# Seven block products for queries and outputs in three attentions, another order of VectorE's work, and weight loads spread over the attentions

## The chip, the cores and the metric

The kernel runs on one core of a Trainium2 chip. The metric is the device time of one execution in microseconds; the time of a version is the median of its runs. The five engines have their names from the profile: PE (TensorE, matmuls; PEld is its weight load), DVE (VectorE), ACT (ScalarE), POOL (GpSimd) and SP (SyncE, which issues most transfers).

## What is computed

Four layers, each of an attention to a fixed context and a feed-forward part, on `x` of 4 batches x 256 tokens x 256 features; the context is 4 x 512 x 128. All is float32. The change concerns the attentions of layers 1, 2 and 3, which are alike:

```python
q = (x @ Wq).reshape(B, 256, 16, 128)          # 16 heads of 128
k = (ctx @ Wk).reshape(B, 512, 8, 128)         # 8, each for two heads
v = (ctx @ Wv).reshape(B, 512, 8, 128)
attn = softmax(einsum('bhtd,bhsd->bhts', q, k) / sqrt(128))
x = x + einsum('bhts,bhsd->bhtd', attn, v).reshape(B, 256, 2048) @ Wo
```

where the `x` in front of `Wq` is layer-normalised. The feed-forward parts are: routed low-rank vectors ("arrows") in layer 0; eight experts, two per token, and a shared one in layer 1; one of two networks per token in layer 2; and in layer 3 a network for the 64 tokens of each batch that a router picks.

## The kernel before

**Folded weights.** `folding` (line 957) multiplies, for each head, Wq with Wk into `m_sb` (256 x 128, as two blocks of 128 rows) and Wv with Wo into `n_sb` (128 x 256). A query is then `m` times the normalised x and is compared with the context itself; the weighted sum of the context times `n` is the output. For each pair of heads it issues eight matmul instructions `pm` (L968), a copy by ACT, the squares of `m` (for a bound on the scores: on POOL with a sum on VectorE for layer 1, on ACT for layers 2 and 3), `pn` (L989) and a copy by VectorE (L992).

**An attention** (line 1674) has 32 units: 4 batches b times 8 pairs of heads hp. The order of work on PE, ACT, DVE and POOL is written out by hand: the engines take their instructions in the order of the program. SP's order is left to the scheduler. In iteration n:

- `queries` of unit n+1 (L1689): for each of 2 heads, two matmuls of 128x128 weights on 256 tokens into one PSUM bank; ACT copies the 128x512 result (L1697).
- `heads` of unit n: four score matmuls of 512 columns (L1704), each followed by ACT's exponential (L1707); four matmuls with the context (L1710); ACT's copy `oT` (L1714); POOL adds two halves of the exponentials (L1717, `half`).
- `quotients`, at hp 1 for the second half of the batch before and at hp 5 for the first half of this one: a matmul `pz` (L1734), VectorE's reciprocal `rz`, and for each of four units VectorE's broadcast `wide` (L1747) and POOL's multiplication of `oT` in place (L1751).
- `summed` of the same unit n: VectorE adds the halves, transposes in blocks of 32 and reduces (L1723, L1725, L1729).
- `output` of the batch before, at hp 3: for each of two token blocks sixteen matmuls of 256 columns (L1760), and VectorE's addition to `x_sb` (L1768).
- `after`: work of the feed-forward part for the batch before, a step at hp 4, 5, 6 and 7 (norm, normalised tokens, transposes, choice of experts; in layer 3 the router, whose matmul `pw`, L2443, takes `diag` from VectorE, L2436).

The norm for the next batch is taken at hp 2, its tokens at hp 4 and its transposes at hp 6. The last batch's outputs stand behind the loop.

PSUM has eight banks in this stage: four for scores (tag "s"), two for "mm" (queries, outputs, folding), one for "o" and one for "t" (transposes, `pz`, small products of the router).

**Loads.** A layer's feed-forward weights are asked for as a block once the raw attention weights have been issued (`issue_after`), at the start of each attention; raw weights of the next attention are issued as four groups at once in the feed-forward part, by `load_raw` (line 941), into pools of two to four buffers.

**Between layers 1 and 2**, experts write their rows to DRAM (`yd`), and class `Back` (line 2162) gathers two rows for each token by indirect transfers of POOL (L2169), which VectorE adds to `x_sb` (L2177). One `Back` is asked for in each step of the folding, with four buffers; the norm of the next attention stands at the fourth step.

**Layer 0's last part** (loop at about line 1617) handles eight blocks of tokens ("arrows"): `routes` on VectorE (L1407 to L1418) with a product on POOL (L1419), transposes (L1427) and outputs (L1436, L1440), the folding of layer 1 in between, and the squares of the context (L1646, L1647).

Of the kernel before, what the change touches and what calls it, by code (L numbers as in the profile page):

```python
# [835 lines left out]
def bounded_path(ctx: ExitStack, tc: tile.TileContext, t, out: bass.AP, over):  # L836
# [30 lines left out]
    def load_fw(tag, shape, parts, name, pool=None):  # L867
        w = (pool or fwp).tile(shape, F32, tag=tag, name=name)
        for dst, src in parts(w):
            nc.sync.dma_start(dst, src)  # L870
        return w

# [68 lines left out]
    def load_raw(L, i):  # L941
# [4 lines left out]
        nc.sync.dma_start(wq_t, wq[h0 * P : (h0 + 4) * P, :].rearrange("(h e) d -> e h d", e=P))  # L946
        wk_t = rawp.tile([P, 2, DC], F32, tag="wk_t", name=f"wk_{L}_{i}")
        nc.sync.dma_start(wk_t, wk[g0 * P : (g0 + 2) * P, :].rearrange("(g e) c -> e g c", e=P))
        wv_t = rawp.tile([P, 2, DC], F32, tag="wv_t", name=f"wv_{L}_{i}")
        nc.sync.dma_start(wv_t, wv[g0 * P : (g0 + 2) * P, :].rearrange("(g e) c -> e g c", e=P))  # L950
        wo_t = rawp.tile([P, 4, D], F32, tag="wo_t", name=f"wo_{L}_{i}")
        done["raw"] = nc.sync.dma_start(
            wo_t, wo[h0 * P : (h0 + 4) * P, :].rearrange("(h e) d -> e h d", e=P)
        ).ins
        raws[L, i] = wq_t, wk_t, wv_t, wo_t

    def folding(L, m_sb, n_sb, on_act=False):

        for i in range(4):
# [4 lines left out]
            for g in range(2):  # L964
# [13 lines left out]
                if on_act:  # L978
                    for h in range(2):
                        nc.scalar.activation(  # L980
                            m2[:, :, h, :], m_sb[:, :, h1 + h, :], AF.Square,
                            accum_out=msq[:, L - 1, h1 + h : h1 + h + 1],
                        )
                else:
                    nc.gpsimd.tensor_tensor(
                        m2, m_sb[:, :, h1 : h1 + 2, :], m_sb[:, :, h1 : h1 + 2, :], ALU.mult
                    )
# [5 lines left out]
                if not on_act:  # L993
                    nc.vector.tensor_reduce(
                        msq[:, L - 1, h1 : h1 + 2], m2.rearrange("p d h c -> p h d c"), AX.XY, ALU.add
                    )
# [21 lines left out]
    with tc.manual_schedule(engines={E.PE, E.Activation, E.DVE, E.Pool}):  # L1018
# [597 lines left out]

        for n in range(B * NC):
            if n + 2 < B * NC:
                arrows[n + 2].routes()
            arrows[n].turned()  # L1620
# [7 lines left out]
            else:  # L1628
# [4 lines left out]
                for _ in range((0, 0, 1, 1, 2, 2, 1, 1)[n]):  # L1633
                    next(fold)
                if n + 3 < B * NC:
# [6 lines left out]
            if 2 <= n < 2 + B:  # L1642
# [4 lines left out]
                nc.vector.tensor_reduce(csq[:, b * NK : (b + 1) * NK], c2, AX.X, ALU.add)  # L1647
# [4 lines left out]
    fwp = ctx.enter_context(tc.tile_pool(name="fwp", bufs=1))  # L1652
# [26 lines left out]

# [1003 lines left out]
```

## Time and profile before

| what | us |
|---|---|
| median of 3 runs | 1537.04 (1534.7 to 1539.55) |
| the profiled execution's own time | 1532.39 |
| its span, first to last instruction | 1530.6 |
| PE busy | 1481.0 (97%) |
| DVE, ACT, POOL busy | 644.9, 589.1, 474.8 |
| VectorE's `summed`: addition, transpose, reduction, 96 each | 782, 711, 686 ns each |
| VectorE's broadcast L1747, 96 | 699 ns each |
| POOL's `half` L1717, 96 | 2344 ns each |
| POOL's division L1751, 90 | 1375 ns each |
| ACT's copies L1697 and L1714, 96 each | 585 ns each |

A row of a group of instructions reads: line, engine, operation, output<-inputs, shape, count, then busy time in us and the mean of one in ns, then the idle time of the engine ahead of them and what ended most of it. Durations of matmuls overlap, since a matmul starts before the one ahead has drained; the distance from start to start is what one costs. The view of waits names engine, line and what it waited for, with the total in us, how often, and the longest. The timeline has start in us, length in us, engine, line. The granted clock is TensorE's, as a share of full speed; over the whole span it was 0.988.

### The profile page before, as it was taken

The page shows a single profiled execution, that of the slowest core. Times are in us where ns is not written, and L with a number is a line of the kernel's source. Part 1 is how long each engine was busy: PE and PEld are TensorE (multiplying, and loading weights), DVE is VectorE, ACT ScalarE, POOL GpSimd, SP SyncE. Part 2 cuts the span into 40 slices and gives each one's busy share as a digit, 9 for nine tenths or more (in the row PEclk, how much of TensorE's full clock was granted, in tenths as well). Part 3 has the DMA queues.
Part 4 walks back from the last instruction along what each step waited for, and adds up shares of the span by engine and source line. Part 5 has one row for each costly group of instructions (what it writes and reads, how often), then busy time and mean ns, then how long its engine had stood idle before and what let it go on. Part 6 is the DMA issues. An engine that isn't in the chain of part 4 may idle for free.

```text
span 1530.6 us, 16401 instructions
## 1 busy us (share of the span) xinstructions
PE 1481.0 (97%) x6243; PEld 935.2 (61%) x6243; DVE 644.9 (42%) x1357; ACT 589.1 (38%) x1047; POOL 474.8 (31%) x354
## 2 busy tenths in 40 slices
PE   8999998999999999999999999999999999999997
PEld 7665676556565567656455656566885565565656
DVE  5666863233534435424233332425442334324363
ACT  4666332442434433234444342422234433423221
POOL 2222343243434331324244342423002343423330
PEclk9999999999999999999999999999999999999999
DMA  4000223100000003135000000000410000000000
GB/s 159 1 1 2 69 69 126 16 0 0 7 1 7 0 3 115 56 86 163 7 0 1 0 1 0 1 0 3 140 55 1 0 1 0 0 1 1 0 0 31
DMA packets 39955, 43.15 MB, mean 28 GB/s; under 512 B 3833, under 2 KB 36826, under 8 KB 39868
## 3 DMA queue, kind: packets, MB, share of 16 engines
q1 hardware_dynamic: 36892, 35.85, 7.4%
q0 software_dynamic: 1872, 5.11, 1.2%
q8 instruction: 52, 0.85, 0.2%
q10 hardware_dynamic: 1104, 1.05, 0.2%
q14 instruction: 35, 0.29, 0.1%
HBM read 36.89 MB, written 5.11 MB: 27 GB/s over the span
## 4 chain that ended last, share of the span: by engine, by line
PE 84%; DVE 9%; POOL 3%; issue 2%; ACT 1%; DMA 0%; POOLq 0%; DVEq 0%; ACTq 0%
PE ps L1704 20%; PE po L1710 20%; PE pq L1689 10%; PE py L1760 10%; PE ph L2308 2%; PE po L2345 2%; PE pgu L2130 2%; PE ps L1313 2%; PE po L1323 2%; PE pyf L1440 1%; POOL oT L1751 1%; PE pyr L2155 1%; PE paf L1390 1%; DVE wide L1747 1%; POOL yg L2169 1%
## 5 line engine op out<-in xcount | busy, mean ns | idle before, releaser
L1717 POOL TENSOR_TENSOR half<-pT 128x1024 f32<-128x1024 f32 x96 | 225.0, 2344 | 579.1 <-ACT pT L1707 406.9
L1704 PE MATMUL ps<-qT,cT 128*128 128x512 f32 x768 | 350.1, 599 | 3.8 <-ACT qT L1697 3.8
L1710 PE MATMUL po<-pT,c_sb 128*128 128x512 f32 x768 | 345.3, 592 | 0.0
L1707 ACT ACTIVATE pT<-ps,mbias 128x512 f32<-128x512 f32 x384 | 263.3, 687 | 77.9 <-PE ps L1704 68.0
L1710 PEld LDWEIGHTS po<-pT,c_sb 128*128 128x128 f32 x768 | 146.0, 190 | 183.6 <-issue 183.1
L1704 PEld LDWEIGHTS ps<-qT,cT 128*128 128x128 f32 x768 | 147.7, 193 | 149.7 <-issue 140.6
L1723 DVE TENSOR_TENSOR half<-half 128x512 f32<-128x512 f32 x96 | 75.0, 782 | 357.4 <-POOL half L1717 357.4
L1689 PE MATMUL pq<-xnT_a,m_sb 128*128 128x256 f32 x768 | 183.4, 383 | 0.7 <-ACT xnT_a L923 0.7
L1760 PE MATMUL py<-n_sb,oT 128*128 128x256 f32 x768 | 169.3, 380 | 1.3 <-POOL oT L1751 1.3
L1689 PEld LDWEIGHTS pq<-xnT_a,m_sb 128*128 128x128 f32 x768 | 143.6, 191 | 39.8 <-issue 14.1
L1760 PEld LDWEIGHTS py<-n_sb,oT 128*128 128x128 f32 x768 | 145.4, 190 | 26.1 <-issue 4.8
L1714 ACT COPY oT<-po 128x512 f32<-128x512 f32 x96 | 56.2, 585 | 263.4 <-PE po L1710 263.4
L1697 ACT COPY qT<-pq 128x512 f32<-128x512 f32 x96 | 56.1, 585 | 255.5 <-PE pq L1689 246.5
L1751 POOL TENSOR_TENSOR oT<-oT,wide 128x512 f32<-128x512 f32 x90 | 121.0, 1375 | 67.3 <-DVE wide L1747 67.3
L1317 ACT ACTIVATE pT<-ps 128x512 f32<-128x512 f32 x128 | 66.1, 603 | 40.8 <-PE ps L1313 40.6
L1747 DVE STREAM_TRANSPOSE wide<-rz 128x512 f32<-128x512 f32 x96 | 65.1, 699 | 28.8 <-POOL oT L1751 28.0
L1725 DVE STREAM_TRANSPOSE turned<-half 128x512 f32<-128x512 f32 x96 | 68.3, 711 | 4.8
L1729 DVE TENSOR_REDUCE sums<-turned 128x16 f32<-128x512 f32 x96 | 65.8, 686 | 3.3
L1743 DVE TENSOR_SCALAR rz<-pz 128x64 f32<-128x64 f32 x24 | 5.4, 224 | 137.1 <-PE pz L1734 137.1
L1768 DVE TENSOR_TENSOR x_sb<-x_sb,py 128x256 f32<-128x256 f32 x24 | 10.1, 421 | 115.9 <-PE py L1760 115.9
L2110 POOL DMA_INDIRECT xg<-xd,who x23 | 22.0, 956 | 59.3 <-PE pxg L2118 33.0
L1313 PE MATMUL ps<-qT,kT 16*128 16x256 f32 x512 | 38.6, 408 | 0.0
(343 smaller groups left out, 1511.3 us busy)
## 6 DMA issues: line engine op xcount, KB each, us to landing
wo<-in_L_wo SPq DMA_DIRECT2D x13, 512.0 KB, 7.1
wq<-in_L_wqT SPq DMA_DIRECT2D x12, 512.0 KB, 4.1
yd<-yr SPq DMA_DIRECT2D x23, 128.0 KB, 1.7
w<-in_F_w SPq DMA_DIRECT2D x2, 1024.0 KB
wgu<-in_F_wgT SPq DMA_DIRECT2D x1, 1760.0 KB, 6.9
wgu<-in_F_wuT SPq DMA_DIRECT2D x1, 1760.0 KB, 10.8
wk<-in_L_wkT SPq DMA_DIRECT2D x12, 128.0 KB, 4.2
wv<-in_L_wvT SPq DMA_DIRECT2D x12, 128.0 KB, 5.9
```

The lines of the kernel that those rows point to most:

```text
L1313: nc.tensor.matmul(ps[j][:, k, :], lhsT=kTs[b][r, hg, k0 : k0 + P], rhs=qTs[b][r, hg, :], start=True, stop=True)
L1317: nc.scalar.activation(pT[kp][:, j], ps[j], AF.Exp)
L1689: nc.tensor.matmul(pq[:, j, :], lhsT=m_sb[:, d, 2 * hp + j, :], rhs=xnTs[b][:, d, :], start=(d == 0), stop=(d == ND - 1),)
L1704: nc.tensor.matmul(ps, lhsT=cT[:, b, k * P : (k + 1) * P], rhs=qTs[b, hp], start=True, stop=True)
L1707: nc.scalar.activation(pT[:, k, :], ps, AF.Exp, bias=mbias[:, b, k : k + 1])
L1710: nc.tensor.matmul(po, lhsT=c_sb[:, b, k, :], rhs=pT[:, k], start=(k == 0), stop=(k == NK - 1))
L1717: nc.gpsimd.tensor_tensor(half, pT[:, 0:2], pT[:, 2:4], ALU.add)
L1723: nc.vector.tensor_tensor(part, half[:, 0], half[:, 1], ALU.add)
L1725: nc.vector.transpose(turned.rearrange("p f i -> p (f i)"), part)
L1747: nc.vector.transpose(wide, rz[:, i, :, None].to_broadcast([P, NB, 32]))
L1751: eng.tensor_tensor(oT, oT, wide.rearrange("p f i -> p (f i)"), ALU.mult)
L1760: nc.tensor.matmul(pys[c], lhsT=outs[b][h // 2][:, t0 : t0 + P], rhs=n_sb[:, h, :], start=(h == 0), stop=(h == H - 1),)
```

## The change

**Seven products.** A product of 2x2 blocks is made with seven block products and sums of blocks, by the scheme of Strassen and Winograd. For queries the blocks are the two 128-row halves of `m` for two heads and two halves of features and of tokens of x; for outputs the two heads and two token blocks of `oT`, and two heads and two feature halves of `n`. Sums of the weights are made once per attention, in its first batch (`m_sums` on VectorE, `n_sums` on POOL, four additions of 128x128 each per head pair), sums of x once per batch (`x_sums`, VectorE), sums of `oT` per unit (`o_sums`, POOL). The fourth of the additions is in place in most cases. The first two units of each attention keep the old form (`first_queries`), and so do the outputs of the last four head pairs of the last batch (`last_output`).

```diff
+            def s_sums(eng, a11, a12, a21, a22, s1, s2, s4):
+                eng.tensor_tensor(s1, a21, a22, ALU.add)
+                eng.tensor_tensor(s2, s1, a11, ALU.subtract)
+                eng.tensor_tensor(s4, a12, s2, ALU.subtract)
+                eng.tensor_tensor(a21, a11, a21, ALU.subtract)
...
+            def seven(of, u, tag="mm", between=None):
+                ps = []
+                for n, which in (("a", (1, 6, 7, 5)), ("b", (2, 3, 4))):
+                    if n == "b" and between:
+                        between()
+                    p = bank(tag, [P, len(which), P], f"p{n}{u}")
+                    for k, pair in enumerate(of):
+                        for at, i in enumerate(which):
+                            lhsT, rhs = pair[i]
+                            nc.tensor.matmul(
+                                p[:, at, :], lhsT=lhsT, rhs=rhs,
+                                start=(k == 0 and at == 0), stop=(k == len(of) - 1 and i == which[-1]),
+                            )
+                    ps.append(p)
+                return ps
+            def four(w, pa, pb):
+                nc.scalar.copy(w[:, 0, :], pa[:, 0, :])
+                nc.vector.tensor_tensor(w[:, 1, :], w[:, 0, :], pa[:, 1, :], ALU.add)
+                nc.vector.tensor_tensor(w[:, 2, :], w[:, 1, :], pa[:, 2, :], ALU.add)
+                nc.vector.tensor_tensor(w[:, 1::2, :], w[:, 1:3, :], pa[:, 3:4, :].to_broadcast([P, 2, P]), ALU.add)
+                nc.vector.tensor_tensor(w[:, 0:3, :], w[:, 0:3, :], pb, ALU.add)
```

The query takes both "mm" banks, an output group two of the four "s" banks. An output group is now four head pairs of one batch (one set of quotients).

**Order in an iteration.** The sums of exponentials of unit n-1 stand before the heads of unit n. Quotients stand at hp 4 (first half of the batch) and hp 0 (second half of the batch before); two divisions each follow at the next two iterations; the output group at the one after.

```diff
+                if n == 0:
+                    first_queries(1)
+                    x_sums(0)
+                elif n + 1 < len(units):
                     queries(*units[n + 1])
+                if b + 1 < B and hp == 6:
+                    x_sums(b + 1)
+                if b == 0:
+                    m_sums((hp + 2) % (H // 2))
+                if n:
+                    summed(*units[n - 1], half)
+                last, i = ((b, 0), hp - 4) if hp >= 4 else ((b - 1, 1), hp)
+                prev = last[0] >= 0
+                h0 = 4 * last[1]
+                if prev and i >= 2:
+                    for k in (2 * i - 4, 2 * i - 3):
+                        o_sums(last[0], h0 + k, nc.gpsimd)
                 half = heads(b, hp)
+                if prev and i == 0:
+                    quotients(*last)
+                if prev and i in (1, 2):
+                    for k in (2 * i - 2, 2 * i - 1):
+                        divided(last[0], h0 + k, nc.gpsimd)
+                if b == 0:
+                    n_sums(hp)
+                if prev and i == 3:
+                    out = Output(*last)
+                    if last != (B - 1, 0):
+                        out.products()
+                        out.add()
                 if after:
                     after(b, hp)
-            output(B - 1, 0, 0, H // 2)
-            quotients(B - 1, 1, last=True)
+            summed(*units[-1], half)
+            out.products(lambda: quotients(B - 1, 1))
+            for k in range(4):
+                divided(B - 1, 4 + k, nc.vector if k % 2 else nc.gpsimd)
+            out.add()
             if at_end:
                 at_end()
-            output(B - 1, 1, 0, H // 2)
-            for c in range(NC):
-                output(B - 1, c, H // 2)
+            last_output(B - 1)
```

The norm of the next batch moves from hp 2, 4 and 6 to hp 1, 3 and 5.

**Loads.** Feed-forward weights are put on a list, and one of them (up to five from the fifth head pair on in layers 2 and 3) is issued on SP after each unit of the first batch, behind ACT's copy of that unit. The down weights of the experts, `wd1` and `wd2`, are issued behind attention 1. Raw weights of layer 2 are issued behind the copies of blocks 2, 8 and 14 of the experts, and a last one after them; of layer 3, two at the start and two behind an addition of batches 0 and 1.

```diff
+    def load_waiting(n=1):
+        for dst, src in waiting[:n]:
+            behind(nc.sync.dma_start(dst, src), done["head"])
+        del waiting[:n]
...
+                if j in (2, 8, 14):
+                    load_raw(2, j // 6, done["slots"])
+            load_raw(2, 3)
```

**Around the attentions.** All squares of `m` are made on ACT; the sum of the context's squares is taken an iteration later; the routes of the last arrow stand behind the folding of iteration 5. Six of eight `Back` are asked for ahead of the folding, the last two after the norm, with eight buffers. ACT's function tables are loaded ahead of their use in three places.

```diff
-            if n + 2 < B * NC:
+            if n + 2 < B * NC and n != 5:
                 arrows[n + 2].routes()
...
+                if n == 5:
+                    arrows[7].routes()
...
+            nc.scalar.preload_act_table_set("exp_and_others")
+            for n in range(N8 - 2):
+                backs[n] = Back(n)
             for n in range(N8):
-                backs[n] = Back(n)
...
+                    for k in (N8 - 2, N8 - 1):
+                        backs[k] = Back(k)
```

## The prediction

> **What bounds the kernel now.** I read the page first, for which engine fills the span, then the groups of instructions, for what fills that engine, then the waits of TensorE, for the rest.
>
> ```profile
> span 1530.6 us, 16401 instructions
> PE 1481.0 (97%) x6243; PEld 935.2 (61%) x6243; DVE 644.9 (42%) x1357; ACT 589.1 (38%) x1047; POOL 474.8 (31%) x354
> ```
>
> ```profile
> L1704 PE MATMUL ps<-qT,cT 128*128 128x512 f32 x768 | 350.1, 599 | 3.8 <-ACT qT L1697 3.8
> L1710 PE MATMUL po<-pT,c_sb 128*128 128x512 f32 x768 | 345.3, 592 | 0.0
> L1689 PE MATMUL pq<-xnT_a,m_sb 128*128 128x256 f32 x768 | 183.4, 383 | 0.7 <-ACT xnT_a L923 0.7
> L1760 PE MATMUL py<-n_sb,oT 128*128 128x256 f32 x768 | 169.3, 380 | 1.3 <-POOL oT L1751 1.3
> ```
>
> TensorE is the bound; no other engine passes 42%. The queries (L1689) and the outputs (L1760), which the change recasts, are 384 matmuls each, shown as x768: a float32 matmul runs as two instructions. Their durations overlap (383 ns each, yet 183.4/768 = 239 ns of busy time), so I price by starts, in the timeline:
>
> ```profile
> 505.58 1.89 PE L1689 MATMUL pq<-xnT_a,m_sb 128*128 128x256 f32 x8
> 507.31 3.60 PE L1704 MATMUL ps<-qT,cT 128*128 128x512 f32 x8
> ...
> 1141.15 1.05 PE L968 MATMUL pm<-wk,wq 128*128 128x128 f32 x8
> 1142.05 1.02 PE L989 MATMUL pn<-wo,wv 128*128 128x512 f32 x2
> ```
>
> Eight instructions of 256 columns take 507.31 - 505.58 = 1.73 us, 216 ns each. L968 has just the shape that the change uses, 128x128 times 128x128 with new weights each time: 0.90 us for eight, 112 ns each. So half the columns cost 0.52 of the time, and a scheme that needs 7/8 of the columns gains less than an eighth. The waits of TensorE are short but not nothing:
>
> ```profile
> PE pw L2443 <- DVE diag L2436: 7.3, 4, 2.8
> PE pn L989 <- DVE n_sb L992: 4.0, 2, 3.8
> PE ps L1704 <- ACT qT L1697: 3.8, 1, 3.8
> PE pxn_f L1887 <- DVE xn_f L908: 1.3, 2, 1.1
> PE pxn_f L2277 <- DVE xn_f L908: 1.3, 2, 1.1
> ```
>
> Some cost more than they show, since TensorE comes back at a lower clock: for 726 to 736 us, after the 3.8 us wait for qT, the view by stretches gives a granted clock of 0.68.
>
> [...]though one LDWEIGHTS shows 191 ns, L968 follows at 112 ns. [...]here 128x1024 (L1717) took 2344 ns, 2.3 ns an element. [...]The divide L1751 (GpSimd, 128x512), with transposes of VectorE beside it, took 1375 ns in place of the 1037 of L985's squares, which have one operand; I take this into the upper bound of the GpSimd price.
>
> **The products.** An attention has 32 units (batch, head pair). All but the first two change from 4 matmuls of 256 columns to 7 of 128; of the 8 groups of four pairs that make outputs, 7 change from 16 of 256 to 28 of 128, the last stays. Over three attentions: 360 + 336 = 696 matmuls go, 630 + 588 = 1218 come. Two instructions each: 1392 x 216 = 300.7 us less, 2436 x 112 = 272.8 us more, **27.8 us gained**. If an interval is 109 ns (transposes with constant weights, L1427) it is 35.2; at 115, 20.6.
>
> **What the sums add, and where they hide.** A unit lasts 1.57 (queries) + 3.43 + 3.43 = 8.4 us on TensorE, and one in four has 56 x 0.112 = 6.3 us of outputs as well: 10 us on average. VectorE: adds of 128, 256, 384 and 512 columns cost 0.28 (L2078, same width), 0.42 (L1768), 0.56 (between), 0.69 (L1351). `four` is 0.28 + 0.28 + 0.42 + 0.56 = 1.5 us a unit, and 2.2 with the residual for each output; m_sums and x_sums are four adds of 0.28, 1.1 us. With the old sums (0.78 + 0.71 + 0.69 = 2.2), a transpose of 0.7 and a norm, that is 5.5 to 7 of 10 us. The result of `four` is wanted a unit later; the copy, four adds and their handing over end about 3 us into the unit, so 5 us of cover; if it went, each us late is a us for each of 90 units. `summed`, put behind it, wants the half of the pair before, which GpSimd gave by then. ACT copies 128 columns instead of 512 (0.585 us), so it is relieved. The output's two banks come from the four of the scores: the third score of the next unit, 1.57 + 1.7 = 3.3 us after the outputs end, wants the first, which VectorE frees before 1 us. Free.
>
> GpSimd has the least room. Per pair it gets four 128x128 operations (o_sums), per pair of the first batch four more (n_sums). No row shows this size with two operands: 256 columns took 733 ns (L1443), the slope up to 1024 is (2344 - 733)/768 = 2.1 ns, so 733 - 269 = **0.46 to 0.5 us**; [...]from above, 0.5 x 1375/1037 = 0.65[...]. Queue, from the start of unit 4 in the first batch, price p: half ends 8.2, n_sums 4p; half of unit 5 starts at 14.3, half and two divides end 19.4, n_sums 4p; o_sums 8p, half and divides 5.1, n_sums 4p; o_sums 8p: the last is there at 24.5 + 24p. TensorE asks for the fourth pair's sums at 36.8. With 0.5 it's 36.5: just no stall. In later batches it's 16.1 + 16p against 27.9: free up to 0.74. I take **1 us** for three first batches; ends 0 and 17.
>
> **Stalls that go.** (1) TensorE's 3.8 us at 233.6 us is the product pn behind an n_sb copy, queued on VectorE behind the router of the last arrow (231.3 to 236.6 us) and two waits for GpSimd's squares. The change puts that router behind the folding, squares to ACT. With the clock of 0.76 in 236 to 243 us, about 1.7 us, it's 5.5; that router is then nearer to its own deadline, so **4.5**; ends 0 and 5.5. (2) The 3.8 us before ps at 726.8 is a copy of qT into memory of the layer before, behind the last add of gathered rows. Gathers stood still from 711.2 to 717.7, behind a norm on GpSimd. Now 12 of 16 go first; last add near 725 rather than 730.1, before TensorE ends its queries (726.9). 3.8 + 5.4 us at half clock = **6.5**; ends 3 and 7. (3) pw waits 1.83 + 1.89 + 2.82 us in attention 3 for diag: VectorE had four broadcasts coupled to GpSimd's divides, then the sums, then the router. Now two broadcasts, the sums before. 6.5 and some 1.5 of slower clock: **7.5**; ends 3 and 8.5. (4) The two longest pxn_f waits, of 1.1 us, have the same cause: **2.2**.
>
> **Stalls that come.** pxg now follows pz directly and shares its single bank: 0.5 us as in pz to pxn_a, three times: **1.4**. At the end of an attention the last sums go through the same chain as before (divides at 586 to 591 us, 0.6 us of wait), beside the outputs of the earlier half: 0. For 422 waits on the new matmuls that should be met when they come: **2**, ends 0 and 8.
>
> **The loads.** SP now takes one weight transfer behind each head pair of a first batch. TensorE waits for no DMA in the trace, so no gain. wd1 and wd2 (1.4 MB) move behind attention 1: the load of 3.5 MB for wgu landed within 11 us (page, part 6), and the experts want them 40 us later. SP queues the xd store behind them, which the gathers want 25 us later. Layer 2's and 3's raw weights wait for a copy or add of the stage; whole blocks of 10 us and more lie before each use. 0.
>
> **Sum.** -27.8 - 4.5 - 6.5 - 7.5 - 2.2 + 1.0 + 1.4 + 2.0 = -44.1. The profiled execution was 1532.4 (span 1530.6); 1488.3. The median of the three runs is 1537.0, 4.6 above it: **1493**.
>
> **The rivals.** *GpSimd late*: at 0.75 us an operation, the queue above gives 24.5 + 18 - 36.8 = 5.7 us of stall in each first batch and 0.2 in 18 later groups, 21 more: 1513. It decides from 0.51 us. For it: halves and divides show that GpSimd is slow and shares. Against: 31% busy. *Edges stay*: the stalls move to the next late thing (the last arrow, the last gathers, the router): only the products and half the rest, 1493 + 10 = 1503, or 1514 with none. *Weights not hidden* (slower): if TensorE can't pull a load ahead past the waits and alternating operands, the 191 ns of a LDWEIGHTS are paid: 2436 x (191 - 112) = 192 us, 1685. It decides from 300.7/2436 = 123 ns. Against it: L968, and outputs of before, which waited on GpSimd as well and went at 216.
>
> **Chances.** Likeliest 0.70 (1480 to 1503), GpSimd late 0.12, edges stay 0.14, weights not hidden 0.04. Low end: interval 109 and the better stalls, 1480. High end 1512: what is left out is half of GpSimd late, a part of no edges, weights, and a little below: under 0.2. 0.3% (5 us) is what a measurement can tell from no change. At 0.82 us an operation GpSimd late would use up the gain (7.4 x 3 + 1.3 x 18 = 45 us); 0.02 of its chance is that, the rest of all but the last case is faster. Faster 0.94, same 0.02, slower 0.04.
>
> **What would show it.** New matmuls at 112 ns start to start; the output group 6.3 us; no wait of ps for DVE; pw, pn and the qT wait gone from the top of TensorE's waits; waits of the output matmuls for GpSimd's ox only at the end of each first batch, under 1 us; 128x128 GpSimd rows near 0.5 us. Wrong if the interval is above 120 ns or ox waits recur in each group.

## The result, and the profile after

| | median us | runs | against the kernel before, 95% interval |
|---|---|---|---|
| before | 1535.87 | 4 | |
| changed | 1495.57 (1490.8 to 1498.36) | 4 | 0.9732 [0.9697, 0.9766] |

The change saves 40.3 us. The profiled execution took 1497.53 us (span 1495.3). The head of its page, and the rows that replace the old queries and outputs:

```profile
span 1495.3 us, 19706 instructions
PE 1451.0 (97%) x7287; PEld 944.8 (63%) x7287; DVE 895.4 (60%) x1940; ACT 573.3 (38%) x1100; POOL 664.6 (44%) x778
...
L1813 PE MATMUL ps<-qT,cT 128*128 128x512 f32 x768 | 345.6, 593 | 0.4 <-ACT qT L1770 0.4
L1819 PE MATMUL po<-pT,c_sb 128*128 128x512 f32 x768 | 345.2, 592 | 0.0
L1783 PE MATMUL paq<-xnT_a,m_sb 128*128 128x128 f32 x360 | 70.7, 278 | 0.1
L1783 PE MATMUL paq<-xx,m_x 128*128 128x128 f32 x360 | 69.8, 275 | 0.0
L1783 PE MATMUL pao<-n_x,ox 128*128 128x128 f32 x336 | 65.0, 275 | 0.0
```

PE executes a thousand instructions more and is busy 30 us less; VectorE went from 42% to 60% and GpSimd from 31% to 44%. The last column is the answer to most of the prediction: the new matmuls wait for next to nothing (0.1 us). Their durations overlap, so the price is again in the starts. One unit in the timeline:

```profile
507.08 0.44 PE L1783 MATMUL paq<-xnT_a,m_sb 128*128 128x128 f32 x2
507.36 0.39 PE L1783 MATMUL paq<-xx,m_x 128*128 128x128 f32 x2
507.58 0.39 PE L1783 MATMUL paq<-xnT_a,m_sb 128*128 128x128 f32 x2
...
508.48 0.39 PE L1783 MATMUL pbq<-xx,m_sb 128*128 128x128 f32 x2
508.70 3.60 PE L1813 MATMUL ps<-qT,cT 128*128 128x512 f32 x8
```

From 507.36 to 508.70 there are 12 instructions: 112 ns each, as the folding's matmuls had promised. The old queries of the same unit took 1.73 us, these 1.62. GpSimd's groups (busy us, mean ns of one, then idle time before them):

```profile
L1860 POOL TENSOR_TENSOR oT<-oT,wide 128x512 f32<-128x512 f32 x90 | 115.5, 1302 | 26.2 <-DVE wide L1859 26.2
L1709 POOL TENSOR_TENSOR ox<-ox,oT 128x128 f32<-128x128 f32 x84 | 46.7, 555 | 6.6
L1708 POOL TENSOR_TENSOR ox<-oT 128x128 f32<-128x128 f32 x84 | 42.3, 503 | 0.0
L1710 POOL TENSOR_TENSOR ox<-oT,ox 128x128 f32<-128x128 f32 x84 | 41.2, 490 | 6.6
L1711 POOL TENSOR_TENSOR oT<-oT 128x128 f32<-128x128 f32 x84 | 38.5, 458 | 0.0
```

The mean of the four is 0.50 us, the estimate's upper value. TensorE's waits, longest first:

```profile
PE pm L983 <- ACT m_sb L991: 6.5, 1, 6.5
PE pz L1845 <- DVE sums L1838: 3.4, 3, 1.8
PE pxn_a L937 <- DVE rz L1854: 2.9, 9, 0.3
...
PE pw L2624 <- DVE diag L2617: 1.3, 1, 1.3
```

The waits for `n_sb` (4.0), for `qT` (3.8, now 0.4) and for `diag` (7.3, now 1.3) are gone, or nearly so. Two others stand in their place. `pz` waits at the three ends of attentions. The first line is one wait of 6.5 us in the folding ahead of attention 2, and no step of the prediction foresaw it:

```profile
702.43 1.02 PE L999 MATMUL pn<-wo,wv 128*128 128x512 f32 x2
...
707.14 0.42 DVE L2155 TENSOR_TENSOR x_sb<-x_sb,pysh 128x256 f32<-128x256 f32 x1 [5.62 <-remote]
709.30 0.60 ACT L991 ACTIVATE m_sb<-pm 128x512 f32<-128x512 f32 x1 [6.98 <-remote]
...
709.95 2.07 PE L983 MATMUL pm<-wk,wq 128*128 128x128 f32 x8 [6.50 <-ACT m_sb L991]
```

Three engines stand still at once. VectorE's addition and ScalarE's copy need only products whose matmuls started at 699.67 and 701.43, and yet they begin at 707 and 709; "remote" says that no event in the profile released them. The semaphore events of PE in the trace come late too (at 707.12 and 709.28), so PE itself was held up, although its matmuls are shown as started. Late instructions are not seen to be the reason: from 695 to 712 us the two queues that carry instructions moved one packet each, as many as in the same stretch of a trace without the stall (690 to 706 us in the second series below).

To see where time goes I cut each trace at the starts of matmuls: the first folding product `pm` of layer 0, and the first and last score matmul `ps` of each attention. The part ahead of `pm` is left out: it has the same PE work in all kernels, but takes 194 to 204 us, since the clock is halved (granted clock 0.50) for one to four stretches in the first 150 us. In the trace of the kernel before that is one of 6.8 us at 29.9 us, and `pm` starts at 194.2 us; in the trace of the changed kernel it is 6.8 us at 20.0 and 13.7 us at 33.7, and `pm` starts at 200.9. One kernel differs from trace to trace as well: the unaltered changed kernel reached `pm` at 200.9, 201.2 and 194.1 us in three of them.

| us from | to `ps` of att. 1 | att. 1 | to att. 2 | att. 2 | to att. 3 | att. 3 | to the last matmul |
|---|---|---|---|---|---|---|---|
| before | 63.3 | 318.7 | 154.8 | 319.7 | 99.5 | 328.8 | 44.8 |
| changed, this trace | 59.0 | 307.7 | 159.4 | 306.0 | 99.5 | 311.1 | 44.9 |
| changed, second series | 59.0 | 307.7 | 149.1 | 306.0 | 99.5 | 311.2 | 45.0 |

The third row is the trace of the changed kernel in the second series of experiments, where the 6.5 us wait is absent. "Series" are kernels run together on one chip; the three series ran on three chips, so I compare times within a series and stages across them. The chip of the result above is not on record.

### The profile page after: what moved, and what is told of

It reads as the page before. It is cut to its first block, busy times and chain, and to the rows that moved or that the text cites. A ratio compares the mean times of both kernels' runs of the same rounds, so it can differ in the third digit from the quotient of the medians.

```text
span 1495.3 us, 19706 instructions
## 1 busy us (share of the span) xinstructions
PE 1451.0 (97%) x7287; PEld 944.8 (63%) x7287; DVE 895.4 (60%) x1940; ACT 573.3 (38%) x1100; POOL 664.6 (44%) x778
## 4 chain that ended last, share of the span: by engine, by line
PE 90%; DVE 6%; POOL 2%; issue 1%; ACT 1%; another core or an unknown queue 0%; POOLq 0%; ACTq 0%; DVEq 0%
PE ps L1813 22%; PE po L1819 21%; PE paq L1783 5%; PE pao L1783 4%; PE pbq L1783 4%; PE pbo L1783 3%; PE ph L2476 2%; PE po L2513 2%; PE pgu L2286 2%; PE ps L1319 2%; PE po L1329 2%; PE pyf L1446 2%; PE py L1896 1%; PE paf L1396 1%; PE pn L999 1%; PE pm L983 1%
## 5 line engine op out<-in xcount | busy, mean ns | idle before, releaser
L1813 PEld LDWEIGHTS ps<-qT,cT 128*128 128x128 f32 x768 | 138.7, 190 | 138.6 <-issue 137.2
L1793 DVE TENSOR_TENSOR qT<-qT,paq 128x128 f32<-128x128 f32 x90 | 25.5, 284 | 90.9 <-ACT qT L1792 90.8
L1793 DVE TENSOR_TENSOR w<-w,pao 128x128 f32<-128x128 f32 x21 | 6.0, 286 | 110.0 <-ACT w L1792 110.0
L1783 PEld LDWEIGHTS paq<-xnT_a,m_sb 128*128 128x128 f32 x360 | 58.0, 191 | 21.5 <-PE po L1819 10.5
L1783 PE MATMUL paq<-xnT_a,m_sb 128*128 128x128 f32 x360 | 70.7, 278 | 0.1
L1783 PE MATMUL paq<-xx,m_x 128*128 128x128 f32 x360 | 69.8, 275 | 0.0
L1783 PE MATMUL pao<-n_x,ox 128*128 128x128 f32 x336 | 65.0, 275 | 0.0
L1792 ACT COPY qT<-paq 128x128 f32<-128x128 f32 x90 | 23.9, 265 | 85.2 <-PE paq L1783 83.1
L1796 DVE TENSOR_TENSOR qT<-qT,pbq 128x384 f32<-128x384 f32 x90 | 49.8, 554 | 9.4
L1783 PEld LDWEIGHTS paq<-xx,m_x 128*128 128x128 f32 x360 | 54.6, 192 | 0.0
```

Of the source, the lines that this page charges most:

```text
L1783: nc.tensor.matmul(p[:, at, :], lhsT=lhsT, rhs=rhs, start=(k == 0 and at == 0), stop=(k == len(of) - 1 and i == which[-1]),)
L1813: nc.tensor.matmul(ps, lhsT=cT[:, b, k * P : (k + 1) * P], rhs=qT, start=True, stop=True)
```

## Experiments

The theory after the result: the products bring what was counted, the order of work brings the stalls at edges, loads nothing; what was not counted is the new wait. The rivals: that the new order of work alone made the gain; that the row of gathers put ahead makes the new wait; that another cause than the one named lay behind a stall.

**Series 1. Old products in the new order.**

```diff
-                four(qTs[b, hp], *seven([of], f"q{L}_{b}_{hp}"))
+                first_queries(hp, b)
...
-                    self.ps = seven(self.of, f"o{self.u}", "s", between)
+                                nc.tensor.matmul(
+                                    py, lhsT=o[:, j * S + c * P : j * S + (c + 1) * P], rhs=n_sb[:, 2 * hp + j, :],
+                                    start=(k == 0 and j == 0), stop=(k == 3 and j == 1),
+                                )
...
-                    x_sums(b + 1)
...
-                    m_sums((hp + 2) % (H // 2))
...
-                        o_sums(last[0], h0 + k, nc.gpsimd)
...
-                    n_sums(hp)
```

> The changed kernel with the old products: every unit's queries are four matmuls of 256 columns, every output group sixteen, and the four kinds of sums (m_sums, x_sums, n_sums, o_sums) and the adds of `four` are left out; the order of the rest, the loads and the folding stay changed. Theory (the products bring 27.8 us and the stalls at edges the rest, separately): 1495.6 + 27.8 = about 1523 us, ratio to the kernel before 0.992; matmuls of 256 columns 216 ns apart again, and the waits for n_sb, qT and diag as short as in the changed kernel. Rival (edges and order made the gain, seven products cost on other engines what they bring on TensorE): 1496 to 1503. Second rival (the products bring more than was counted, since the old form also waited elsewhere): 1530 or more.

Measured: 1509.68 us, 0.9862 [0.9838, 0.9885]. Its stages: 59.0, 316.5, 150.5, 314.8, 98.6, 319.2, 44.6. The matmuls of 256 columns start 216 ns apart again, and the waits for `n_sb`, `qT` and `diag` are as short as in the changed kernel. So both halves are real and separate: everything but the products (order, loads and the work around the attentions together) saves 21.2 us (17.6 to 24.8) of 1533.5, and seven products shorten the attentions by 8.8, 8.7 and 8.0 us before rounding, 25.5 in all. From the intervals I expect 30 x (8 x 216 - 14 x 112) ns + 6 x (32 x 216 - 56 x 112) ns = 8.64 us for each such stretch (the seventh output group lies behind its last score). The kernel is 24.6 us slower than the one with the early router in the same series, 1.5 of which are the router's. The forecast of its time, 1523 and a ratio of 0.992, missed, since I had set it on the 1495.6 that the new wait is part of. One of the waits of `pz` is there without the products as well:

```profile
PE pz L1839 <- DVE sums L1832: 2.0, 1, 2.0
```

**The gathers by step again.**

```diff
-            for n in range(N8 - 2):
-                backs[n] = Back(n)
             for n in range(N8):
+                backs[n] = Back(n)
...
-                    for k in (N8 - 2, N8 - 1):
-                        backs[k] = Back(k)
```

> The changed kernel, with the gathers of the experts' rows for layer 2 issued one per step of the folding again, in place of twelve in a row ahead of it. Theory A (the row of gathers, together with the weight load of layer 2, makes the new wait of 6.5 us at 703 us): that wait is gone, the 3.8 us wait for qT near 727 us with its slower clock is back; the two cancel, 1491 to 1498 us. Theory B (the wait at 703 us was one event of one execution and has nothing to do with the gathers): the other kernels of this call, which keep the row, show no such wait in their traces, and this kernel is 4 to 7 us slower than they would be, 1500 to 1503 us.

Measured: 1492.2 us, 0.9734 [0.9715, 0.9754]. The wait for `qT` is back:

```profile
PE ps L1813 <- ACT qT L1770: 3.6, 1, 3.6
PE pz L1845 <- DVE sums L1838: 3.4, 3, 1.9
```

The way to attention 2 with attention 2 took 157.3 + 308.9 = 466.2 us, against 455.2 for the changed kernel in series 2; 5.1 of the 11.0 are lost in a stretch of half clock at 608 us, so the gathers are worth about 6 us, where the prediction had 6.5. The time itself lies in theory A's range, but both ranges had been set on the 1495.6. What separates the theories is that no other kernel of this series has the wait at 703 us, though they keep the row of gathers: that is theory B's sign, and the row is not enough to make the wait.

**The router of the last arrow in its old place.**

```diff
-            if n + 2 < B * NC and n != 5:
+            if n + 2 < B * NC:
...
-                if n == 5:
-                    arrows[7].routes()
```

> The changed kernel, with the router of the last arrow at its old place, ahead of two steps of the folding in layer 0; the squares stay on ScalarE. Theory: the wait of the product pn for the n_sb copy near 233 us is back with 3 to 4 us, and a slower clock behind it; about 1500 us (+4.5). Rival (moving the squares off GpSimd had cured it alone): no change, 1494 to 1497 us, the wait under 1 us.

Measured: 1485.09 us, 0.9693 [0.9672, 0.9713]. My theory falls: no wait of `pn`, and the first stage takes 57.5 us instead of 59.0. The router's move was not the cure; it costs 1.5 us, the 1.3 us wait of `puTf` for GpSimd's `twof` that this kernel no longer has.

**The sums in the unit that made them, and four divides at once.**

```diff
-                if n:
-                    summed(*units[n - 1], half)
...
-                if prev and i in (1, 2):
-                    for k in (2 * i - 2, 2 * i - 1):
+                if prev and i == 1:
+                    for k in range(4):
                         divided(last[0], h0 + k, nc.gpsimd)
...
+                summed(b, hp, half)
...
-            summed(*units[-1], half)
```

> The changed kernel, with the sums of exponentials again in the unit that made them (behind its divides), and the four divides of a quarter in one unit in place of two and two. Theory (this order caused the waits for diag in attention 3 and the longest ones for xn_f): the three waits of pw for diag are back with some 2 us each, the ones of pxn_f with 1 us; 1495.6 + 7.5 + 2.2 = about 1505 us. Rival (VectorE is now at 60 percent, so that sums ahead of the adds of `four` make ps wait for qT in many of 90 units, up to 1 us each): 1515 to 1580 us. Second rival (seven products have changed VectorE's load so much that the old place is as good): 1494 to 1498 us.

Measured: 1523.61 us, 0.9937 [0.9921, 0.9953]: nearly the whole gain is gone. The attentions take 317.0, 315.2 and 328.4 us. The size is the rival's, the place isn't: `ps` hardly waits for `qT`; the new products wait for their sums.

```profile
PE paq L1783 <- DVE xnT_a L1717: 9.5, 5, 2.3
PE paq L1783 <- DVE xx L1715: 5.3, 2, 2.6
PE paq L1783 <- DVE m_x L1709: 4.4, 3, 1.5
```

Why a sum is late shows in one of them, in the timelines of VectorE, GpSimd and TensorE:

```profile
406.28 0.43 DVE L1716 TENSOR_TENSOR xx<-xnT_a,xx 128x128 f32<-128x128 f32 x1
406.64 2.42 DVE L1717 TENSOR_TENSOR xnT_a<-xnT_a 128x128 f32<-128x128 f32 x1
408.99 0.94 DVE L1832 TENSOR_TENSOR half<-half 128x512 f32<-128x512 f32 x1
```

```profile
406.53 2.38 POOL L1826 TENSOR_TENSOR half<-pT 128x1024 f32<-128x1024 f32 x1
```

```profile
409.12 0.49 PE L1783 MATMUL paq<-xnT_a,m_sb 128*128 128x128 f32 x2 [2.31 <-DVE xnT_a L1717]
```

An addition of 0.28 us takes 2.42 us, and TensorE waits 2.31 us for it. The addition starts 0.1 us after GpSimd's `half` and ends 0.15 us after it (409.06 against 408.91). In this trace eight such additions take over 2 us, and each ends 0.15 us behind a `half`. Both inputs of these additions are in SBUF. The additions of `four` that have one input in PSUM are not held up: in the trace of the changed kernel twelve of them lie wholly within a `half` and take at most 0.29 us. Being held up is not yet a loss, though. The changed kernel itself has two such additions, in attention 3, of which this is one; no wait of TensorE for them appears in its list, and by the starts the matmul that uses it comes some 0.3 us late:

```profile
1270.73 2.32 DVE L1715 TENSOR_TENSOR xx<-xnT_a,xx 128x128 f32<-128x128 f32 x1
```

It counts when TensorE asks for the sum before the `half` has ended. Not all of this kernel's waits are of this kind: for `m_x` (1.5 us in each attention) VectorE was late, with its additions at about 0.5 us each.

**Series 2. One more GpSimd operation in each set of sums.**

```diff
                 eng.tensor_tensor(s4, a12, s2, ALU.subtract)
+                if eng is nc.gpsimd:
+                    eng.tensor_tensor(s4, a12, s2, ALU.subtract)
...
                 eng.tensor_tensor(t4, b21, t2, ALU.subtract)
+                if eng is nc.gpsimd:
+                    eng.tensor_tensor(t4, b21, t2, ALU.subtract)
```

> The changed kernel, with one more GpSimd operation of 128x128 (the third one repeated) in every o_sums and n_sums: five in place of four a pair. Theory (the queue of the prediction: GpSimd is just in time in a first batch and has 4 us of room in the others, 1.25 us in two groups of attention 3): in a first batch six sets of sums lie ahead of the last one that TensorE wants, 6 x 0.49 = 2.9 us, three times 8.8; in the other groups 4 x 0.49 = 2.0 us, hidden, but for two times 0.7: about 10 us more than the changed kernel, ratio to the kernel before 0.980, all of it as waits of pao or pbo for ox or oT in the first output group of an attention. Rival A (GpSimd's work hinders VectorE[...] in every pair): 20 us or more, spread. Rival B (the first batch has room after all): no change, ratio 0.973.

Measured: 1507.14 us, 0.9826 [0.9797, 0.9856], 20.7 above the unaltered kernel of this series.

```profile
PE pz L1849 <- DVE sums L1842: 9.6, 3, 4.0
PE pao L1787 <- POOL oT L1713: 6.3, 8, 1.0
```

The second line is the theory: six of the eight waits, 1.0 us each, lie in the first output group of the three attentions; the other two, of 0.2 us, are in attention 3. With the shorter waits that this view leaves out, attentions 1 and 2 are 3.2 us longer each, and attention 3 is 4.8 longer, 1.7 of it in a stretch of half clock: 9.5 in all, where 8.8 was expected for the three first groups. In the unaltered kernel the last sums of those groups end 0.17 us after TensorE asks for that pair, and 3.4 to 4.2 us ahead of it in most others. The first line I had not expected: the extra work delays the last `half` of an attention, and `pz` waits 9.6 us at the three ends, in place of 3.4. The 20.7 us are rival A's amount, but not its mechanism.

**The loads at once.**

```diff
-        if b == 0:
-            load_waiting()
+        if b == 0 and hp == 0:
+            load_waiting(len(waiting))
...
-            load_waiting(1 if hp < 4 else 5)
+            load_waiting(len(waiting) if hp == 0 else 0)
```

> The changed kernel, with all waiting weight loads of an attention issued behind its first head pair, in place of one behind each head pair. Theory (loads are hidden either way): no change, ratio to the kernel before within 0.003 of the changed kernel's in this call. Rival (the spread keeps the memory traffic from slowing the engines in a first batch): 3 to 10 us slower, and waits or longer operations in the first tens of us of the attentions.

Measured: 1489.11 us, 0.9706 [0.9679, 0.9734]. Stages 59.0, 307.7, 150.8, 306.0, 99.5, 311.2, 44.9: as the unaltered kernel but for 1.7 us at a stretch of half clock at 614 us. The loads are hidden either way.

**The changed kernel again.** No edit.

> The changed kernel once more, unaltered, beside the others of this call and for a second trace. Theory (the wait of 6.5 us at 703 us was one event of one execution): the trace has no such wait, the way from the end of attention 1 to the start of attention 2 takes 153 to 154 us in place of 159.4, the median is 1486 to 1490 us if the event is rare. Rival (it comes back in most executions of just this kernel, by the timing of its gathers and its weight load): the wait is there again, 1491 to 1497 us.

Measured: 1486.46 us (1482.08 to 1487.77), 0.9679 [0.9650, 0.9707], without the wait at 703 us.

**The last sums on VectorE, and the router early.**

```diff
+                if (b, hp) == units[-1]:
+                    nc.vector.tensor_tensor(half[:, 0], pT[:, 0], pT[:, 1], ALU.add)
+                    nc.vector.tensor_tensor(half[:, 0], half[:, 0], pT[:, 2], ALU.add)
+                    nc.vector.tensor_tensor(half[:, 0], half[:, 0], pT[:, 3], ALU.add)
+                    return half
...
-                nc.vector.tensor_tensor(part, half[:, 0], half[:, 1], ALU.add)
+                if (b, hp) != units[-1]:
+                    nc.vector.tensor_tensor(part, half[:, 0], half[:, 1], ALU.add)
```

The other edit is that of the router, as in series 1.

> The changed kernel with two edits: the router of the last arrow at its old, earlier place, and the sums of exponentials of an attention's last head pair made by VectorE alone, in three adds of 512 columns, two of which can be done before the last exponential, in place of one GpSimd add of 1024 columns (2.35 us) and one VectorE add. Theory: the end of each attention has a chain exp, half, summed, pz; it gets some 2.4 us shorter, and the three waits of pz for the sums, 2.0 + 1.0 + 0.9 us, go: about 4 us below the run with the early router alone, 1481 us (ratio 0.967). Rival (the wait moves to the divides that follow pz, or VectorE is late with the adds of the output group): 1484 to 1487 us, a wait of py for oT or of pz in their place.

Measured: 1479.67 us (1479.22 to 1483.2), 0.9646 [0.9619, 0.9673], the best of all kernels.

```profile
PE pz L1849 <- DVE sums L1842: 1.1, 1, 1.1
```

Two of the three waits are gone. The one at attention 1's end is 1.1 instead of 1.9: there VectorE's transposition of the sums stands behind the choice of experts (568.1 to 571.3 us), as its addition did in the unaltered kernel, and not behind GpSimd. Against the unaltered kernel the stages gain 1.5 (router), 1.0 between attentions 2 and 3 and 1.0 at the end; between 1 and 2 it is 148.3 against 149.1, once 3.4 us for a stretch of half clock are taken off. That is 4.3 us; the rest of the 6.8 us between the medians is not in these stages; the start, which varies between traces of one kernel too (194.1 to 201.2 us), differs by 3.1 us in the two traces.

**Series 3. The four divides alone, and the sums alone.** The two parts of series 1's last kernel, each by itself.

> The changed kernel, with only the four divides of a quarter in one unit again (the sums of exponentials stay a head pair later). Theory (what cost 31 us in the run with both parts undone is that VectorE stands in front of `summed`, waiting for GpSimd's half of the same pair): 0 to 6 us more than the changed kernel of this call, ratio 0.968 to 0.972. Rival (it is the four broadcasts, coupled to GpSimd's divides by two buffers, that hold VectorE): most of the 31 us, ratio 0.982 or more.

> The changed kernel, with only the sums of exponentials back in the unit that made them, behind the divides; the divides stay two and two. Theory: 25 to 31 us more than the changed kernel, ratio 0.984 to 0.989, as waits of the new query matmuls (paq) for x_sums, m_sums and `four` of VectorE, spread over the attentions. Rival (the four divides carry the loss): 0 to 8 us more, ratio at most 0.974.

Measured: 1501.91 us, 0.9767 [0.9755, 0.9780], and 1503.6 us, 0.9778 [0.9752, 0.9804], against 1497.43 for the unaltered kernel of this series: 4.5 and 6.2 us. Neither carries the loss. The cost forecast for the divides (0 to 6 us) holds, though not its ratio, since the unaltered kernel of this series is slower too; the theory that the sums carry the loss falls, and so does its rival. In series 1 the two together cost 37 us (1523.6 against 1485.1 and 1.5 for the router); in attentions 1 and 2 that is 9 us each in the traces, where the divides alone cost under 0.1 and the sums alone 0.3. In attention 3 the divides alone cost 10.8 us (322.0): two additions of x_sums are held up for 2.3 us behind `half`, TensorE waits 2.6 us for each, and the clock is halved for 10 us after them.

```profile
PE paq L1783 <- DVE xx L1715: 5.2, 2, 2.6
```

In the second kernel eight sums are held up for 2.2 to 2.5 us just as in the combined one, yet only two of them make TensorE wait, 0.8 us each, in attention 3. This is the one that was shown above for the combined kernel; it ends at 393.82 us, and the matmul that uses it starts at 393.87 without a wait:

```profile
391.38 2.44 DVE L1717 TENSOR_TENSOR xnT_a<-xnT_a 128x128 f32<-128x128 f32 x1
```

What differs is that TensorE comes to them later in VectorE's work: VectorE has not also stood 3.5 us before a broadcast for GpSimd's divide. I infer this from the two traces; no run isolates it. The 6.2 us are a loose figure: this kernel's six executions lie between 1494 and 1508 us, and its traced one, among the fastest, loses 2.6 us in the three attentions.

**The changed kernel, third time.** No edit.

> The changed kernel unaltered for a third time. Theory (the first measurement, 1495.6 us, held an event that is rare; 1486.5 us is the usual time): 1484 to 1489 us, ratio 0.966 to 0.970, no wait at 703 us. Rival (the time moves by such an amount from one series to the next): 1490 us or more.

Measured: 1497.43 us (1493.5 to 1497.99), 0.9736 [0.9720, 0.9751]. The stall is back, in another shape: PE stands with nothing to wait for.

```profile
698.28 1.46 PE L2151 MATMUL pysh<-wds,gsT 128*128 128x256 f32 x6
703.69 2.07 PE L983 MATMUL pm<-wk,wq 128*128 128x128 f32 x8 [3.94 <-issue]
```

All four kernels of this series have it, at 697 to 710 us; the seven kernels of series 1 and 2 with the same row of gathers don't. In this trace the stage takes 163.1 us against 149.1; about 4 us of it are this wait, and four stretches of half clock between 572 and 709 us (20.4 us, half of it lost) are the rest. "Rare event" falls, and "timing of this kernel", the rival of the run before, falls as well; what holds is that the time moves by such an amount from one series to the next. The last group of layer 2's raw weights was moving in the trace of the result; in this one its data come only from 704 us, after the stall began, so that load isn't the cause either.

The medians say one thing more. The kernel before took 1536.15 us in series 2 and 1537.47 in this one, 1.3 more, while the unaltered changed kernel took 11.0 more. So the kernel before does not pay this stall on the chip where the changed one does, although it was not traced there.

**The squares of layer 0's folding on GpSimd again, router early.**

```diff
-                for h in range(2):
+                for h in range(2 if L > 1 else 0):
...
+                if L == 1:
+                    nc.gpsimd.tensor_tensor(
+                        m2, m_sb[:, :, h1 : h1 + 2, :], m_sb[:, :, h1 : h1 + 2, :], ALU.mult
+                    )
...
+                if L == 1:
+                    nc.vector.tensor_reduce(
+                        msq[:, L - 1, h1 : h1 + 2], m2.rearrange("p d h c -> p h d c"), AX.XY, ALU.add
+                    )
```

> The changed kernel, with the router of the last arrow at its old place (which alone cost nothing) and the squares of layer 0's folding on GpSimd again, with VectorE's reductions of them. Theory (the squares made the wait of pn near 233 us: VectorE stood in front of its reductions, waiting for GpSimd): the wait of pn for n_sb is back with 3 to 4 us, the way from the first folding product to the first scores of attention 1 takes 62 to 63 us in place of 57.5 with the squares on ScalarE; 4 to 6 us more than the run with the early router. Rival (the earlier place of the reductions of the context's squares in the old kernel was part of it): under 60 us, no such wait.

Measured: 1498.56 us, 0.9740 [0.9712, 0.9767], with the stall of this series. The first stage takes 57.5 us, exactly as with the squares on ScalarE; the theory falls again. What remains of the change in that loop is the reduction of the context's squares (`csq`), which the changed kernel makes a step later. VectorE at the last arrow's router, in the kernel before and in this one:

```profile
230.63 0.69 DVE L1647 TENSOR_REDUCE csq<-c 128x4 f32<-128x512 f32 x1 [1.83 <-POOL c L1646]
231.25 1.21 DVE L1407 TENSOR_REDUCE nrf<-twof 128x64 f32<-128x1024 f32 x1
...
236.89 0.68 DVE L992 COPY n_sb<-pn 128x512 f32<-128x512 f32 x1
```

```profile
231.88 1.21 DVE L1421 TENSOR_REDUCE nrf<-twof 128x64 f32<-128x1024 f32 x1
...
237.21 0.68 DVE L1637 TENSOR_REDUCE csq<-c 128x4 f32<-128x512 f32 x1
...
238.14 0.69 DVE L1006 COPY n_sb<-pn 128x512 f32<-128x512 f32 x1
```

Before, VectorE stood 1.83 us ahead of this reduction for a GpSimd product just issued, and the router with it. Now the reduction stands behind the router, and the product is long there. Counted from the first `pm` (194.2 us before, 200.9 here), the router starts at 37.1 us before and at 31.0 here, and the copy `n_sb` that `pn` needs at 42.7 and 37.2. About 2.5 of the 6.1 us lie directly in front of this router; the rest had come about in the same way at the two routers ahead of it, at 12.4 and 23.2 us against 9.9 and 19.6. So with the router and the squares in their old places and this reduction alone deferred, the wait of `pn` does not come back. The reverse, the reduction alone in its old place, was not run.

## Why the prediction was right, step by step

The time was predicted at 1493.0, and 1495.57 came out, inside the range. That it came so close is partly luck. The sum of savings (44.1) was somewhat small, and a stall that it didn't contain made up for it: where the stall is absent (series 2), the change brings 49.7 us; where it is present, 40.0 to 40.3.

| step of the sum | predicted | measured |
|---|---|---|
| products | -27.8 | -25.5 between first and last scores (25.9 expected there); size right |
| (1) `pn` at 233 us | -4.5 | -4.3 (63.3 to 59.0); cause wrong |
| (2) gathers, wait for `qT` | -6.5 | about -6 by the run with gathers by step |
| (3) `diag` in attention 3 | -7.5 | -9.6 (328.8 to 319.2 with old products) |
| (4) `pxn_f` | -2.2 | the two waits are gone, and two of 0.2 us beside them |
| GpSimd late in first batches | +1 | under 0.2 each |
| `pxg` behind `pz` | +1.4 | 0.6 shown, twice 0.3 |
| waits on the new matmuls | +2 | 0.1 (rows of L1783); their mean interval is 112.5 ns |
| end of attention | 0 | 3.4 of wait for `pz`, 1.4 more than with old products |
| loads | 0 | 0 |
| stall at 697 to 710 us, half clock behind it | not seen | about +8.6 in the trace of the result (10.3 less 1.7 for a half clock at 614 us); also in series 3 |

**The products** went as worked out. The central assumption was that a weight load of 191 ns stays hidden behind running matmuls, as at L968, also under alternating operands. The loads of L1783 take 191 to 192 ns on average, and its matmuls start 112 ns apart without a wait, so the rival *Weights not hidden* falls.

**GpSimd's queue** was the closest call and the best hit: worked out at 36.5 us against a demand at 36.8, the trace has the last sums 0.17 us after the demand for their pair, and a fifth operation makes each first batch 3.2 us longer. *GpSimd late* was near, not far; its price of 0.75 us an operation was my estimate, and no trace shows it (0.50 us measured). One reading behind its upper price was wrong. The divides L1751 are not slowed by VectorE's transposes: 42 of them with only transposes beside them took 1.26 to 1.28 us, as those with nothing beside them in the trace after. The mean of 1375 ns comes from 21 that began under VectorE's addition of halves (L1723), which has two SBUF inputs; these took 1.71 to 1.74 us.

**Step (1)** had its size and not its reason. I named the router's place and the squares. The router put back alone, and both put back together, left no stall; the deferred reduction of the context's squares, which I had read in the diff and not priced, is enough. The timeline of before had the 1.83 us in front of that reduction; the prediction spoke of the router and of GpSimd's squares only. The router's move, which I had credited with part of the saving, costs 1.5 us. That the size came out is luck.

**Step (3)** was under-sized by the clock: attention 3 of the kernel before holds two stretches of half clock (at 1385 and 1474 us, 3.4 us each, half of which is lost), and I had added 1.5 us for them. They begin behind waits of 1.89 and 2.82 us; behind the wait of 1.83 us in the same attention the clock was not halved.

**The end of an attention**, costed at nothing because the chain was the same as before, was the term without cover: `pz` is now wanted 0.8 to 1.9 us before its sums are ready. The run with a fifth operation lengthens these waits, and the one with VectorE's last sums removes two of the three. In four of the fourteen traces (those with the old products, the early router, the fifth operation, and the third of the changed kernel) a stretch of half clock of 3.4 us also begins within 1.4 us of the wait at attention 1's end, so in some executions it may cost 1.7 us more than it shows.

**The stall at 700 us** stays open. It isn't in the program's waits, it doesn't come from the row of gathers alone nor from the raw load, and in the three series it went with the chip. By its times the kernel before doesn't pay it there; whether the kernel with gathers by step does was not tried. The rival *Edges stay* fell otherwise: the stalls that it kept are gone, and the kernel with old products, which keeps the rest of the change, saves 21.2 us.

## What to carry to other kernels

Price a matmul by its start-to-start interval in the stage where its shape already runs, not by its row's mean duration (here 112 ns against 275 to 278); then a 7-for-8 scheme is seen to be worth 25 of the 301 us of matmuls that it recasts, a twelfth and not an eighth. A scheme that moves work to other engines lives by its order: put first what the bound engine waits for, let an engine consume what another made a unit ago, and keep VectorE operations with two SBUF inputs that the bound engine is about to ask for off the time of long GpSimd operations (here such an addition of 0.28 us took up to 2.47 us beside one of 2.34 to 2.40 us). When a stall has several candidates in one diff, undo each alone before naming the cause; here the two that were named were innocent.

## What the runs showed of the hardware that was not expected

- A VectorE addition of two 128x128 SBUF operands, 0.28 us, took up to 2.47 us when it began beside a GpSimd addition of 1024 columns (2.34 to 2.40 us), and in each of the 37 cases over 2 us, in eleven traces, it ended 0.15 us after that.
- On one chip of the three series, PE stood still for 4 to 8 us at the same place of the program in four of four kernels (and in the trace of the result, whose chip is not on record), with late semaphores and no cause in the profile. The seven kernels with the same row of gathers on the two other chips don't show it.
- The stretches of half clock (3.4 to 13.7 us) in the first 150 us move the start of the same product by up to 10 us: it came at 194.0 to 204.4 us in the fourteen traces, and at 194.1 to 201.2 in three of one kernel.
